# Early rows of x, late constant rows, and a new order in a planned attention layer

## The chip, the cores and the metric

The kernel runs on one core of a Trainium2 chip. The core has a matrix engine (TensorE, PE in the profile, with its weight loads shown apart as PEld), a vector engine (VectorE, DVE), a scalar engine (ScalarE, ACT), a general engine (GpSimd, POOL) and SyncE (SP), which issues the transfers between main memory and the core's own memory. The metric is device time in microseconds (us) from the first to the last instruction of one execution, with a little around it; lower is better.

## What is computed

The input x has 8 rows (batch) of 1024 tokens and 256 channels, all in float32. The layer is a chain of four blocks, each added to its input after a layer norm:

```python
x = x + retention(layernorm(x))     # 4 heads, dk 64, dv 128, gated, rotary, decay per head
x = x + ffn(layernorm(x))           # token shift, sigmoid(r) * (relu(k)^2 @ W_v)
x = x + attention(layernorm(x))     # 16 heads of 16, full softmax, bias by distance
x = x + ffn(layernorm(x))           # the same weights once more
```

The retention is a recurrent block. Per chunk of tokens, `attn = (q @ k.T) * Dmask` is applied to v, a state S of 64 x 128 per head carries what came before, the result is normed per head, gated with `g * sigmoid(g)` and multiplied by `Wo`. The feed-forward block mixes each token with the one before it, `xr = mu_r * x + (1 - mu_r) * x_prev` and the same for xk, and computes `sigmoid(xr @ W_r.T) * (relu(xk @ W_k.T)**2 @ W_v.T)`. The attention adds to each score a bias `rel_bias[bucket(distance)]`, which is the same for all keys far enough away, and takes a softmax over all 1024 keys.

## The kernel before

**Rows and chunks.** The eight rows go through the same functions, `retention(b)`, `ffn_front(b)`, `project_b(b)`, eight pairs of heads in `maxima(b, j)` and `shift(b, j)`, four groups of heads in `weigh(b, g)`, and `back(b)`. A row is cut into `NC = 4` chunks of `CT = 256` tokens; retention works on eight blocks of 128 tokens. `prepare(c)` loads a chunk of x and takes its moments; `turn_chunk(c)` norms it (tile z), turns it on PE and makes two float32r parts nT of it (line 912 writes the second, on DVE in the first row). A product that needs more than float32r's precision is three float32r matmuls of such parts (`mm3`, line 646); the projections qps, vps and gps of retention and qkp and bvp of attention are made so. The feed-forward and output products are plain float32.

**The attention** puts each head's queries and keys into stacks in main memory, `stk[0]` and `stk[1]`. Beside the 16 channels, a head's stack holds constant rows: for the queries, rows that say which key block a token may see as far (`c_stat`, copied from memory to memory by two transfers, lines 773 to 777), and for the keys, the same pattern times the head's far bias. The latter are worked out in the function `later()`: a tile `stat` is loaded, `d31` and `d0` hold two rows of the bias table, `fac` is made from them by a few small DVE instructions, and for each of the 16 heads DVE multiplies `stat` by a column of `fac` into a tile `kr` (line 798), which is stored into both parts of the key stack (line 800). The tiles stat and kr use the five buffers of the tag "k", the same as the key stacks loaded by `load_pair` later. `maxima` finds each query's greatest score, `weigh` computes the exponentials (tile e) and their products with the values (acc), and `back` divides by the sums, multiplies by the output weights (bop) and runs the second feed-forward block, `ffn_chunk(xt, b, c, "g", "")`.

**The feed-forward block** (`ffn_chunk`, line 1114) has one buffer each for zT, xk and xr per lane; the lane's name is the last argument. `ffn_front` uses the lane "f", `back` the lane "". In a chunk, the difference between a token and the one before is written into xk, then xr and xk are computed from it (lines 1130 to 1132), xk last and in place. kps is the keys' product, xk then takes its relu and its square, rps is the receptance product, whose tanh is written into xr, and yps the last product. xr then takes the product of both, and is added to x.

**The start.** SP's first transfers are a table of constants (cm), the norm's weights (ln), the four pieces of Wq and Wk (through the staging tiles xo, in `split`, which makes two float32r parts on ACT and DVE), and then the first chunk of x. `next_ones()` loads and splits Wv and Wg, loads Wo; `later()` loads all other weights and the constant rows.

**The order of the work** is not that of the text. Every operation is recorded (`Plan.record`) with an engine, an estimated cost and a target; `issue` then runs a clock of its own and lets each engine take, among the operations whose inputs are ready by that clock, the one with the lowest target (plus, for PE, penalties). What comes out is a fixed list for each engine, and the engines follow their lists in order. Targets run from -1 for the first row's retention up by one per row; `later()` is recorded at -0.9. Three things steer the order beside the targets: the estimate of a transfer,

```python
op.cost, op.tail = 0.4, 2.0 + size / 100000.0
```

the estimate of a matmul in `mm` (line 643), and the penalties. PE pays for a change in how its array is used ("rows" for the score products with 64 contracted rows, "cols", "acc", "all"). How much the choice counts such a change, and how much room for results it demands, is one of 16 `RULES`; the string `TURNS` names the rule, one hexadecimal digit for each 20 us of the planned clock.

```python
rule = RULES[int(TURNS[min(int(now / STRETCH), len(TURNS) - 1)], 16)]
change, least, pairs, later = rule[0], rule[1], rule[2], rule[3:]
```

Almost all instructions are emitted by `Plan.emit`, so the profile puts them at line 608; they are told apart by the names of their tiles. One plain float32 matmul appears as two instructions.

Of the kernel before, what the change touches and what calls it, by code (L numbers as in the profile page):

```python
# [76 lines left out]

STRETCH = 20
TURNS = (
    "00070270877472bf8931ef967bfe1d0522ff04383dfe37be3f1f7ef668e19e9c33271224f3e73df5"  # L80
    "5663e6176b19fd77763fbb3cafd79ff9fb9bf84111"
)
SWITCH = 0.1

# [227 lines left out]
class Plan:  # L312
# [66 lines left out]
    def record(self, eng, real, method, args, kw):  # L379
        cost = kw.pop("cost", None)  # L380
        views = [a for a in list(args) + list(kw.values()) if isinstance(a, View)]
        outs = [kw[k] for k in ("out", "accum_out") if isinstance(kw.get(k), View)]
        if "out" not in kw and isinstance(args[0], View):
            outs.append(args[0])
        if method in ("matmul", "transpose"):
            out, group = outs[0].t, kw.pop("group", None)
            op = self.last
            if op is None or op.group is not group or group is None and op.out[0] is not out:
                op = self.new(eng)
                op.out, op.cost, op.group = [], 0.0, group  # L390
                self.last = op
                k, m = args[1].shape[0], 1
                for n in args[1].shape[1:]:
                    m *= n
                op.mode = ("rows" if k == 64 and m == P else "cols") if k == 64 or m == 64 else "all"
                if out.tag == "acc":
                    op.mode = "acc"
                op.late = (0.055 if method == "transpose" else 0.1) if op.mode == "all" else 0.0
            if out not in op.out:
                op.out.append(out)  # L400
            op.cost += cost
        else:
            op = self.new(eng)
            n = 1
            for v in views:
                m = 1
                for d in v.shape[1:]:
                    m *= d
                n = max(n, m)
            if method == "dma_start":  # L410
                size = 4
                for d in (args[0] if isinstance(args[0], View) else views[0]).shape:
                    size *= d
                op.cost, op.tail = 0.4, 2.0 + size / 100000.0
            else:
                op.cost = self.estimate(eng, method, n, views, {
                    **kw, "op": args[3] if len(args) > 3 else None,
                    "scalar": len(args) > 2 and isinstance(args[2], View),
                })
                op.tail = AFTER[eng]  # L420
        op.calls.append((real, method, args, kw))
        for v in views:
            if v.t.space != "in":
                self.touch(op, v, any(v is o for o in outs))
        return op
# [186 lines left out]
def layer_kernel(ctx: ExitStack, tc: tile.TileContext, ap: dict, out: bass.AP):  # L612
# [26 lines left out]
    def mm(o, lhsT, rhs, start=True, stop=True, share=1.0, group=None):  # L639
        n = 1  # L640
        for d in rhs.shape[1:]:
            n *= d
        pe.matmul(o, lhsT, rhs, start=start, stop=stop, group=group,
                  cost=share * (0.004 + (4 if rhs.dtype == F32 else 1) * max(n, 64) / 2400.0))

    def mm3(o, lhsT, rhs, first, last):

# [24 lines left out]
    def split(w, names):  # L672
        for c in range(ND):
# [4 lines left out]
            act.copy(w[0][:, c], t)  # L678
            dve.tensor_tensor(w[1][:, c], t, w[0][:, c], ALU.subtract)

    split(wqk, ("a_Wq", "a_Wk"))
    wo_a = const([P, RH, D], "wo_a")
    gn = const([P, 1], "gn")
# [49 lines left out]
    def later():  # L733
        sp.dma_start(mu, ap["f_mu"])
        for k, t in wf.items():
            sp.dma_start(t, ap["f_" + k].rearrange("(c p) n -> p c n", p=P))

        dve.tensor_scalar(wf["W_v"], wf["W_v"], 0.5, None, ALU.mult)
        for k, w in wb.items():
            t = tile2k("xo0", 2).rearrange("p (c n) -> p c n", c=ND)  # L740
            sp.dma_start(t, ap["b_" + k].rearrange("(c p) n -> p c n", p=P))

            by = AHD**-0.5 if k == "wq" else 1.0
            act.activation(w[0], t, AF.Copy, scale=by)
            dve.scalar_tensor_tensor(w[1], t, by, w[0], ALU.mult, ALU.subtract)
        sp.dma_start(wo_b, ap["b_wo"].rearrange("(c p) n -> p c n", p=P))
        sp.dma_start(bqk, ap["b_bqk"])
        dve.tensor_scalar(bqk[:, 0, :], bqk[:, 0, :], AHD**-0.5, None, ALU.mult)

        rel = small([NBUCK, AH], "rel", 1)  # L750
        sp.dma_start(rel, ap["b_rel"])
        hot = tile2k("xo1", 2)
        sp.dma_start(hot[:NBUCK, :NU], ap["c_hot"])
        ups = misc("ups")
        mm(ups[:AH, :NU], rel, hot[:NBUCK, :NU])
        usb = tile2k("xo1", 2)
        dve.tensor_copy(usb[:AH, :NU], ups[:AH, :NU])
        sp.dma_start(ud, usb[:AH, :NU])


        bv, bo1 = small([P, ND], "bv", 1), tile2k("ob")[0:1, :D]
        sp.dma_start(bv, ap["b_bv"])
        sp.dma_start(bo1, ap["b_bo"])
        bps = misc("bps")
        for c in range(ND):
            mm(bps[0:1, :D], bv[:, c : c + 1], wo_b[:, c], c == 0, c == ND - 1)
        dve.tensor_tensor(bo1, bo1, bps[0:1, :D], ALU.add)
        sp.dma_start(bd, bo1)
        sp.dma_start(bo, bd.raw(0, [[0, P], [1, D]]))


        c_stat = ap["c_stat"]
        for i in range(2):
            sp.dma_start(
                stk[0][i, ROW_SHIFT // AHD],
                bass.AP(tensor=c_stat.tensor, offset=c_stat.offset, ap=[[0, AH], [T, AHD], [1, T]]),
            )
        stat = plan.tile([P, T], F32, "k", "stat", NJ)
        sp.dma_start(stat[:NSTAT], c_stat[1])
        far = small([NSTAT, NPART + 1], "far", 1)  # L780
        sp.dma_start(far, ap["c_far"])
        d31, d0 = small([NSTAT, AH], "d31", 1), small([NSTAT, AH], "d0", 1)
        sp.dma_start(d31, ap["b_rel"][NBUCK - 1].partition_broadcast(NSTAT))
        sp.dma_start(d0, ap["b_rel"][0].partition_broadcast(NSTAT))
        dve.tensor_tensor(d31, d31, d0, ALU.subtract)

        fac = small([NSTAT, AH], "fac", 1)
        dve.tensor_scalar(fac, d31, 0.0, far[:, NPART : NPART + 1], ALU.mult, ALU.add)
        for part in range(NPART):
            db = small([NSTAT, AH], f"db{part}", 1, F32R)  # L790
            dve.tensor_copy(db, d31)
            dve.tensor_tensor(d31, d31, db.bitcast(F32), ALU.subtract)
            dve.scalar_tensor_tensor(
                fac, db.bitcast(F32), far[:, part : part + 1], fac, ALU.mult, ALU.add
            )
        for h in range(AH):
            kr = plan.tile([P, T], F32, "k", "kr", NJ)[:NSTAT]
            dve.tensor_scalar(kr, stat[:NSTAT], fac[:, h : h + 1], None, ALU.mult)
            for i in range(2):
                sp.dma_start(stk[1][i, ROW_SHIFT // AHD, h], kr)  # L800

    def swift(alone):

# [70 lines left out]
    def retention(b):  # L874
        norms = {}

        def prepare(c):

            t = tile2k("xc", 4).rearrange("p (n d) -> p n d", n=2)
            sp.dma_start(t, rows_in(x[b], c))  # L880
            xc[b, c] = t
            mv = moments(t, "a")

# [230 lines left out]
    def ffn_chunk(xt, b, ch, name, own):  # L1114
# [11 lines left out]
        prev, cur = zT[:, :, 0:CT], zT[:, :, 1 : CT + 1]  # L1126
        xk = plan.tile([P, ND, CT], F32, "xk" + own, "xk", 1)
        xr = plan.tile([P, ND, CT], F32, "xr" + own, "xr", 1)
        eng.tensor_tensor(xk, cur, prev, ALU.subtract)
        for i, t in ((0, xr), (1, xk)):  # L1130
            for c in range(ND):
                dve.scalar_tensor_tensor(t[:, c], xk[:, c], mu[:, i, c : c + 1], prev[:, c], ALU.mult, ALU.add)
        lasts[name, b, ch] = small([P, ND, 1], name + "_last")
        pool.tensor_copy(lasts[name, b, ch], zT[:, :, CT : CT + 1])
        kps = misc("kps").rearrange("p (d t) -> p d t", d=ND)
# [34 lines left out]
    def project_b(b):  # L1170

        for ch in range(NC):
# [10 lines left out]
            for s, w in ((0, "wq"), (1, "wk")):  # L1183
# [15 lines left out]
                swift(b == 0).tensor_tensor(pt[1], res, pt[0], ALU.subtract)  # L1199
                t0 = (NC - 1 - ch if s == 0 else ch) * CT  # L1200
                for p, i in enumerate((Q_PARTS, K_PARTS)[s]):
                    sp.dma_start(rows_of(s, b, t0, p), pt[i].bitcast(F32))
            vps = misc("bvp")
            for i in range(2):
                for c in range(ND):
# [27 lines left out]
    def two(ps, q, k, qc, kc, queries):  # L1233

        group = object()
        for hh in range(2):
            r = slice(hh * HROWS, (hh + 1) * HROWS)
            a, m = (k[r, kc], q[r, qc]) if not queries else (q[r, qc], k[r, kc])
            mm(ps[hh] if isinstance(ps, list) else ps[:, hh, :], a, m, share=0.525, group=group)

    def near_bias(j, tag, bufs):

# [142 lines left out]
    def back(b):  # L1385

        for c in range(NC):
# [21 lines left out]
                       k == 0, k == ND - 1)  # L1409
            xf = xt.rearrange("p n d -> p (n d)")  # L1410
            dve.tensor_tensor(xf, xf, bps, ALU.add)
            ffn_chunk(xt, b, c, "g", "")
            sp.dma_start(rows_in(out[b], c), xt)


    for b in range(B):
# [3 lines left out]
            later()  # L1420
        ffn_front(b)
        project_b(b)
        for j in range(NPAIR):
            maxima(b, j)
            shift(b, j)
# [24 lines left out]
```

## Time and profile before

The median of the runs is 2560.08 us, the lowest 2556.73. The profiled execution took 2558.84 us, of which the span from the first to the last instruction is 2557.1.

| what | value |
|---|---|
| PE busy | 2474.7 us, 97% |
| DVE, ACT, POOL busy | 2108.6, 2071.8, 1592.5 us |
| mean granted clock of PE | 0.993 of full speed |
| DMA over the span | 251.17 MB, 98 GB/s |
| PE busy in 0 to 20, 20 to 40, 40 to 60 us | 2.91, 11.98, 14.82 us |
| PE busy in 2500 to 2520, 2520 to 2540, 2540 to the end | 15.69, 15.86, 8.27 us |
| first useful projection (qps) begins | 29.48 us |
| first query store (stk<-qk) is issued | 100.82 us |
| first loads of the stacks (q<-stk, k<-stk) are issued | 194.40 us |
| last value product (acc) ends | 2503.3 us |

A row of the timeline reads: start, duration (both in us), engine, line, operation, what it writes <- what it reads, shapes, and how many instructions are merged; in brackets, how long the engine was idle before and what ended the wait. A row of waits reads: who waited <- for whom: us in total, times, longest. A row of the chain reads: start, duration, what. Engines work beside each other, so that an engine's busy time is not the run's time; idle time counts where it is PE's.

### The profile page before, as it was taken

To read this page: it belongs to the slowest core of one execution; us is meant where nothing else is said; L and a number is where in the kernel's file an instruction comes from. 1 tells how busy PE (TensorE), PEld (TensorE's weight loads), DVE (VectorE), ACT (ScalarE), POOL (GpSimd) and SP (SyncE) were. 2 spreads that over 40 slices of the span, in tenths; PEclk is the share of its full clock that TensorE was granted. 3 is DMA by queue.
4 is the path that set the end of the run, shared out by engine and by line. 5 is a ranking of instruction groups with operands and counts; after the bars stand their busy time and mean duration, and the time that the engine had idled before them with its cause. 6 is when DMAs were issued, how large, how long until landed. Compare 5 with 4: busy or idle time off the path is not lost.

```text
span 2557.1 us, 51506 instructions
## 1 busy us (share of the span) xinstructions
PE 2474.7 (97%) x15814; PEld 1458.3 (57%) x15814; DVE 2108.6 (82%) x6230; ACT 2071.8 (81%) x5334; POOL 1592.5 (62%) x2675
## 2 busy tenths in 40 slices
PE   5999999999999999999999999999999999999997
PEld 3887755555555555555555555555555555554455
DVE  6767998888888888988888788888888888888855
ACT  3565598888989888988888889888898888787883
POOL 3467666666756666666657576666666566666642
PEclk9999999999999999999999999999999999999999
DMA  7136322444334333332324333324233344443322
GB/s 175 45 106 150 81 59 67 130 108 111 84 106 105 85 99 101 110 98 79 92 63 119 98 105 101 98 73 109 72 98 93 94 119 121 120 122 106 95 63 67
DMA packets 252225, 251.17 MB, mean 98 GB/s; under 512 B 89043, under 2 KB 226181, under 8 KB 251925
## 3 DMA queue, kind: packets, MB, share of 16 engines
q1 hardware_dynamic: 251956, 247.89, 36.6%
q8 instruction: 132, 2.16, 0.4%
q14 instruction: 137, 1.11, 0.2%
HBM read 151.32 MB, written 98.59 MB: 98 GB/s over the span
## 4 chain that ended last, share of the span: by engine, by line
PE 79%; DVE 9%; DMA 5%; ACT 4%; POOL 2%; issue 2%; SPq 1%; POOLq 0%; DVEq 0%; ACTq 0%
PE acc L608 16%; PE p L608 10%; PE s L608 10%; PE kps L608 4%; PE wps L608 4%; PE yps L608 4%; PE rps L608 4%; DVE pm L608 3%; PE qkp L608 3%; PE vps L608 3%; PE qps L608 3%; PE gps L608 3%; PE ops L608 3%; ACT e L608 2%; PE bop L608 2%
## 5 line engine op out<-in xcount | busy, mean ns | idle before, releaser
L608 DVE TENSOR_REDUCE pm<-p 128x1 f32<-128x512 f32 (+2 forms) x2048 | 1058.0, 558 | 84.9 <-PE p L608 83.1
L608 ACT ACTIVATE e<-s 128x512 f32<-128x512 f32 (+2 forms) x2048 | 1006.4, 526 | 54.9 <-PE s L608 51.8
L608 POOL TENSOR_TENSOR e<-e,hk 128x512 f32<-128x512 f32 (+1 forms) x558 | 615.0, 1109 | 344.9 <-ACT e L608 330.5
L608 PE MATMUL acc<-e,va 128*17 128x512 f32 x4096 | 529.0, 599 | 3.2 <-ACT e L608 2.9
L608 DVE CUSTOM_DVE_ANT_0 jmax<-p,hk 128x256 bf16<-128x256 f32 (+1 forms) x1152 | 428.1, 372 | 112.9 <-PE p L608 108.0
L608 PE MATMUL p<-k,q 64*128 64x512 f32 x2048 | 460.8, 439 | 5.4 <-DVE pm L608 3.1
L608 ACT COPY e<-s 128x256 f32<-128x256 f32 (+1 forms) x1116 | 398.9, 357 | 82.4 <-PE s L608 80.3
L608 PE MATMUL s<-q,k 64*128 64x512 f32 x2048 | 457.2, 438 | 5.4 <-DVE pm L608 3.3
L608 ACT ACTIVATE e<-e 128x512 f32<-128x512 f32 (+1 forms) x576 | 336.0, 586 | 56.4 <-POOL e L608 53.3
L608 PEld LDWEIGHTS p<-k,q 64*128 64x128 f32 x2048 | 207.9, 185 | 249.1 <-ACT e L608 95.2
L608 PEld LDWEIGHTS s<-q,k 64*128 64x128 f32 x2048 | 206.2, 185 | 204.4 <-issue 68.6
L608 PEld LDWEIGHTS acc<-e,va 128*17 128x17 f32 x4096 | 77.8, 95 | 189.0 <-issue 161.0
L608 PE MATMUL rps<-W_r,xr 128*128 128x256 f32 x512 | 127.7, 392 | 12.0 <-DVE xr L608 10.4
L608 PE MATMUL yps<-W_v,xk 128*128 128x256 f32 x512 | 126.9, 391 | 4.6 <-DVE xk L608 3.4
L608 PE MATMUL kps<-xk,W_k 128*128 128x256 f32 x512 | 128.1, 393 | 2.0 <-DVE xk L608 1.0
L608 PE MATMUL wps<-wo_a,gs 128*128 128x256 f32 x512 | 125.7, 388 | 0.6 <-ACT gs L608 0.5
L608 PEld LDWEIGHTS rps<-W_r,xr 128*128 128x128 f32 x512 | 93.3, 192 | 44.5 <-issue 12.4
L608 PE MATMUL qps<-wqk,nT 128*128 128x512 f32 x384 | 107.0, 414 | 6.0 <-DVE nT L608 5.5
L608 PEld LDWEIGHTS kps<-xk,W_k 128*128 128x128 f32 x512 | 94.3, 192 | 30.9 <-issue 10.7
L608 PEld LDWEIGHTS yps<-W_v,xk 128*128 128x128 f32 x512 | 93.1, 191 | 32.6 <-issue 12.1
L608 PEld LDWEIGHTS wps<-wo_a,gs 128*128 128x128 f32 x512 | 92.5, 190 | 26.5 <-issue 4.7
L608 POOL TENSOR_TENSOR ao_y<-ao_a,mhalf 128x4 f32<-128x4 f32 x64 | 65.7, 1027 | 66.6 <-DVE ao_a L608 65.9
(182 smaller groups left out, 4180.4 us busy)
## 6 DMA issues: line engine op xcount, KB each, us to landing
stk<-qk SPq DMA_DIRECT2D x192, 256.0 KB
hk<-ud SPq DMA_DIRECT2D x128, 256.0 KB
q<-stk SPq DMA_DIRECT2D x128, 256.0 KB
k<-stk SPq DMA_DIRECT2D x128, 256.0 KB
od<-o SPq DMA_DIRECT2D x64, 256.0 KB
vd<-vst SPq DMA_DIRECT2D x64, 136.0 KB
va<-vd SPq DMA_DIRECT2D x32, 272.0 KB
xc<-in_x SPq DMA_DIRECT2D x32, 256.0 KB
```

Of the source, the lines that this page charges most:

```text
L608: getattr(real, method)(*[be(a) for a in args], **{k: be(a) for k, a in kw.items()})
```

## The change

The first chunk of x is loaded by a transfer that is recorded ahead of the weights' (tile `first`). The constant rows of the stacks leave `later()` for a function `constant_rows()`, called after the first row's projections with the target -0.6, and all its transfers are planned behind the first query store (`stored[0]`). In the last row's `back`, odd chunks use the lane "f" and even ones the lane "", the difference is written into xr instead of xk, and xk is computed first. The plan's estimates change: transfers of operations with a target below -0.85 are taken to run at half the rate, float32r matmuls to cost n / 2270 us instead of n / 2400, and the pair of score products 0.5 of a matmul each instead of 0.525. The string of rules is another one. No other instruction is added or removed.

```diff
 TURNS = (
-    "00070270877472bf8931ef967bfe1d0522ff04383dfe37be3f1f7ef668e19e9c33271224f3e73df5"
-    "5663e6176b19fd77763fbb3cafd79ff9fb9bf84111"
+    "01721211a7731e138937018e991bcf6a3080107fffb91fb9013e97538778092d97bffb24e3e5d77e"
+    "efefa7f8fe786ec03266f72d4d1b1ff3f39caffb111"
 )
...
-                op.cost, op.tail = 0.4, 2.0 + size / 100000.0
+                op.cost, op.tail = 0.4, 2.0 + size / (50000.0 if self.target < -0.85 else 100000.0)
...
-                  cost=share * (0.004 + (4 if rhs.dtype == F32 else 1) * max(n, 64) / 2400.0))
+                  cost=share * (0.004 + (4 * max(n, 64) / 2400.0 if rhs.dtype == F32 else max(n, 64) / 2270.0)))
...
+    first = plan.tile([P, HALF], F32, "xc", "xc", 4)
+    sp.dma_start(
+        first.rearrange("p (n d) -> p n d", n=2), x[0][:CT, :].rearrange("(n p) d -> p n d", p=P)
+    )
     split(wqk, ("a_Wq", "a_Wk"))
...
+    stored = []
+
+    def constant_rows():
+
+        start = len(plan.ops)
+        plan.target = -0.6
         c_stat = ap["c_stat"]
...
+        for op in plan.ops[start:]:
+            if op.eng == "SP":
+                op.before.add(stored[0])
...
-            t = tile2k("xc", 4).rearrange("p (n d) -> p n d", n=2)
-            sp.dma_start(t, rows_in(x[b], c))
+            t = (first if b == c == 0 else tile2k("xc", 4)).rearrange("p (n d) -> p n d", n=2)
+            if b or c:
+                sp.dma_start(t, rows_in(x[b], c))
...
-        eng.tensor_tensor(xk, cur, prev, ALU.subtract)
-        for i, t in ((0, xr), (1, xk)):
+        diff = xr if name == "g" and b == B - 1 else xk
+        eng.tensor_tensor(diff, cur, prev, ALU.subtract)
+
+        for i, t in ((1, xk), (0, xr)) if diff is xr else ((0, xr), (1, xk)):
             for c in range(ND):
-                dve.scalar_tensor_tensor(t[:, c], xk[:, c], mu[:, i, c : c + 1], prev[:, c], ALU.mult, ALU.add)
+                dve.scalar_tensor_tensor(t[:, c], diff[:, c], mu[:, i, c : c + 1], prev[:, c], ALU.mult, ALU.add)
...
-                    sp.dma_start(rows_of(s, b, t0, p), pt[i].bitcast(F32))
+                    stored.append(sp.dma_start(rows_of(s, b, t0, p), pt[i].bitcast(F32)).n)
...
-            mm(ps[hh] if isinstance(ps, list) else ps[:, hh, :], a, m, share=0.525, group=group)
+            mm(ps[hh] if isinstance(ps, list) else ps[:, hh, :], a, m, share=0.5, group=group)
...
-            ffn_chunk(xt, b, c, "g", "")
+
+            ffn_chunk(xt, b, c, "g", "f" if b == B - 1 and odd else "")
...
         project_b(b)
+        if b == 0:
+            constant_rows()
```

## The prediction

> **What bounds the kernel now.** I read the page's engine rows first, then PE's own waits over the whole run, then the busy times by stage, and last the order of instructions at the two ends.
>
> ```profile
> span 2557.1 us, 51506 instructions
> PE 2474.7 (97%) x15814; PEld 1458.3 (57%) x15814; DVE 2108.6 (82%) x6230; ACT 2071.8 (81%) x5334; POOL 1592.5 (62%) x2675
> PE   5999999999999999999999999999999999999997
> ```
>
> PE is the bound: 97% busy, and in the slices only the first and the last are not full. All of PE's idle time is 2557.1 - 2474.7 = 82.4 us, which caps what a better order can bring, apart from changes of PE's own work. The waits say where the largest pieces lie (total, times, longest):
>
> ```profile
> PE bps L608 <- DMA bv<-in_b_bv: 17.0, 1, 17.0
> PE rps L608 <- DVE xr L608: 10.4, 6, 3.3
> PE qps L608 <- DVE nT L608: 5.5, 1, 5.5
> PE ops L608 <- ACT S L608: 5.2, 1, 5.2
> PE bop L608 <- POOL ob L608: 5.0, 1, 5.0
> ```
>
> Rows one, three and four are the head, row two is almost all the tail. By stage PE is busy 2.91 of the first 20 us, 11.98 of the second and 14.82 of the third: 30.3 us idle before 60 us. From 2500 to the end it is busy 15.69 + 15.86 + 8.27 = 39.8 of 57.1: 17.3 us idle. What is between, 60 to 2460 us, has 2365.45 of 2400 busy: 34.6 us idle in 2400.
>
> **The head: the first rows of x and the constant rows.** The order of the first useful matmul's inputs:
>
> ```profile
> 8.62 0.75 DVE L608 BATCH_NORM_STATS2 a_st<-xc 128x6 f32<-128x256 f32 x2
> ...
> 16.81 1.09 ACT L608 ACTIVATE z<-xc,a_nb,a_y 128x256 f32<-128x256 f32 x2
> ...
> 20.91 1.02 ACT L608 ACTIVATE z<-ntp,ln 128x256 f32<-128x256 f32 x2
> ...
> 25.66 0.16 DVE L608 TENSOR_TENSOR d<-d,d 16x16 f32<-16x16 f32 x1 [5.70 <-DMA d<-in_b_rel]
> ...
> 28.75 0.67 DVE L608 TENSOR_TENSOR nT<-z,nT 128x512 fp32r<-128x512 f32 x1
> ...
> 29.48 2.93 PE L608 MATMUL qps<-wqk,nT 128*128 128x512 f32 x6 [5.50 <-DVE nT L608]
> ```
>
> The second nT part needs z, ready at 21.93, but starts at 28.75: DVE stands for 5.70 us at the constant rows' first subtraction, whose two small loads were issued (17.94 to 18.96) behind two 1 MB copies of constant rows (14.31 and 16.28). That is 28.75 - 21.93 = 6.8 us, and these instructions leave the head. The step before it, z at 16.81, could have started when a_nb ended (13.89 + 0.20 = 14.09), but ACT stood at the second gate weight's load: 2.7 us. The doubled cost of early transfers makes the planner expect those weights later, so z should go first. The x load itself is SP's seventh issue (3.60) and becomes the third (1.70): 1.9 us earlier for x, and the four weight loads that it passes go 0.47 us later each. DVE read x at 8.62, directly behind the weight subtraction of 8.01 to 8.70; with x third it can read it at about 5.5 (the first pair of weight loads, issued at 2.18 to 2.61, was there at 5.59, about 3.0 us later). That is 3.1 us. Sum 6.8 + 2.7 + 3.1 = 12.6: the first projection at about 17 instead of 29.5.
>
> Less than that reaches the end. After 29.48 PE still idles 30.52 - 25.34 = 5.2 us up to 60, nearly all of it at ops, whose S copy stood on DVE behind constant rows; but with one row's retention alone its steps depend on each other, so I keep half of it and some 2 us of other waits (DVE still has weights to split, and stands 3.1 us at bqk). I take **-10 us**, with ends -2 (only x's earlier issue counts) and -15 (12.6 plus half of 5.2).
>
> PE's clock bears on this: from 50 to 60 us it is 0.75, behind the 5.2 us gap, and in the tail eight rps matmuls behind a 2.72 us gap take 3.38 us where those of the chunk before take 1.97. [...]
>
> **The same work, later.** Moved are 2 copies of 1 MB, 4 small loads, 32 stores of 64 KB (38 issues on SP), on DVE 16 kr at 0.734 = 11.7 us and eight small instructions, 1.5 us. They stand behind the first query store, issued at 100.82 before and some 10 us earlier now. Their deadline is far: the first q and k loads are at 194.4. In 95 to 145 us DVE is busy 35.3 of 50 and the DMA engines 0.40, so there is room; but PE has 48.75 of 50, and every DVE instruction there feeds it. The price is bounded below by 0 (all in DVE's 14.7 us of idle time). Above, take DVE standing 5.7 us at d once more, 0.8 at kr's buffers and half the 13.2 us of work in PE's way: 12. SP stood for kr 8.8 us in seven waits; the second chunk's stores and x loads (stk at 131, xc at 134) are queued behind, with some 30 us to spare. I take **+4**, nearer to the lower end because the rows on either side of the window show DVE at 70%.
>
> [...] POOL's 0.20 us steps take 0.63 at 2511.77, beside a DVE subtraction of two SBUF inputs. [...] No row shows a kr beside a busy POOL chain.
>
> **The tail: two lanes and keys first.** The chain that ended last:
>
> ```profile
> 2539.18 2.01 PE yps L608 x8
> ...
> 2542.54 0.69 DVE xk L608
> ...
> 2543.89 3.38 PE rps L608 x8
> 2547.27 1.74 PE kps L608 x8
> ...
> 2549.03 0.61 ACT xk L608
> ...
> 2549.66 0.70 DVE xk L608
> ...
> 2550.41 2.01 PE yps L608 x8
> ...
> 2553.17 0.69 DVE xo L608
> ```
>
> The last chunk's zT is ready at 2538.30 + 0.58 = 2538.88, but its xk waits until the third chunk is through yps, xr and xo: 2542.54. With its own buffers it starts 3.7 us earlier. Keys first put relu and square (0.61 + 0.70) beside rps: 1.3 us. Without the gap, rps is not at the slow clock: 1.4. Together 6.4. Further back, the third chunk's bop stood behind the first's yps (2521.22 against a product ready at 2519.94) and the last chunk's ftp behind kps (2537.60 against z at 2536.30): 1.3 each, of which I count half. Against it: the difference now lies in xr, which is free only after the final addition, not after yps; for the first chunk that is 2513.62 instead of 2511.66, but it is not on the path, since the third chunk waits for the sums' loads (2519.2). 6.4 + 1.3 = 7.7: **-8**, with ends -3 (the lane's 3.7 alone, less 0.7 should xr's wait reach the last chunk) and -9 (6.4 + 2.6).
>
> **The middle: new turns and rates.** The string picks one of 16 rules per 20 us of planned time; almost every instruction may stand elsewhere. Costs of two() hardly change: 0.525 x (0.004 + 512/2400) = 0.1141 becomes 0.5 x (0.004 + 512/2270) = 0.1148. Unshared float32r becomes 5% dearer in the plan, 0.2295 for 512 columns, and six of them measure 1.39 / 6 = 0.232. That is a truer plan, and no instruction is faster. What the rules steer is how often PE changes its array use: two s matmuls take 0.43, four 0.66, so a change costs 0.2. From PE's order I counted the changes per 20 us stretch from 360 to 2400 us: 15.5 to 18.0, by the old digit. The new digits with these means give 1694 changes against 1699: 1 us. So I take **0**. Bounds: the 34.6 us of idle time and some 14 us of slow clock (six 100 us stretches at 0.97 to 0.98) might shrink by 20, or grow by half, 25: they lie where a batch's transfers crowd (DMA share 0.82 at 2190 to 2200, bop idle 5.0, clock 0.76) and where the new order meets them is open.
>
> **Sum.** -10 + 4 - 8 + 0 = -14. The profiled execution took 2558.84 us (span 2557.1 and 1.7 around it), so 2544.8; the median of the runs is 1.2 us above it, which is less than I can claim. Forecast **2545**.
>
> **Rivals.** (1) *The middle gains too*, as the truer plan keeps PE fed: the same ends and -20 in the middle, 2525. For it: 48 us are lost there; against: the count of changes stands still. (2) *Slower than before*: PE, which takes its instructions in order, meets transfers that land later than planned, at the joints of the batches. Price by the place at 2190 to 2202: 5.0 us idle, then bop 3.80 instead of 1.92, and the clock still 0.90 in the next 10 us: 8 us each. Six such dips of the clock exist now (at 1220, 1430, 1530, 2070, 2190 and 2340); two more eat the 14 us, four more give 2545 + 32 = 2577, and it decides from the second on. (3) *The x load doesn't do what it says*: z stays behind weights on ACT and nT behind other waits on DVE, as it stood behind bqk and ups; the head gives -2, the moved rows cost 4, the tail 8: 2553.
>
> Chances: forecast 0.55 (2530 to 2556 with its own bounds), (1) 0.18, (2) 0.17, (3) 0.10. The range takes in (1), (3) and the nearer half of (2): 2520 to 2570. A difference under 2%, 51 us, can hardly be told from none in measurements of this kernel: faster than that 0.04, within 0.92, slower 0.04.
>
> **What would show it.** In the profile after, the first qps near 17 us and the first 60 us with some 20 us idle; no d or kr on DVE before 80 us, and PE no worse than 97% busy from 90 to 140; kps ahead of rps in the last chunks, and the last xo ending some 43 us behind the last acc, where it is 2553.9 - 2503.3 = 50.6 now. I am wrong if PE stands near 100 us for DVE, or if idle time between 60 and 2460 us moves by over 20 us.

## The result and the profile after

The change made the kernel a little slower: 2569.54 us median of five runs (2564.97 to 2579.0) against 2557.68 before, a ratio of 1.0053 with a 95% interval of 1.0034 to 1.0071; the ratio leaves out one of the five runs of before, 2720.51 us, which was in a slower state. That is 9 to 18 us more, where 14 fewer were forecast. The profiled execution took 2564.97 us, of which the span is 2563.3.

The page of the kernel after, its span, the engines' busy times and PE's slices:

```profile
span 2563.3 us, 51511 instructions
PE 2481.1 (97%) x15814; PEld 1463.0 (57%) x15814; DVE 2108.7 (82%) x6230; ACT 2069.4 (81%) x5334; POOL 1590.5 (62%) x2675
PE   6899999999999999999999999999999999999997
```

PE's idle time is 82.2 us, as before (82.4), and PE is busy 6.4 us longer for the same 15814 matmuls. So idle time changed its place. The mean granted clock is 0.993 in both, so the page alone doesn't say which matmuls took longer; from 100 to 150 us the clock is 0.90, where it was 1.00. The first slice is fuller (6 where it was 5). PE's waits in the kernel after (total, times, longest):

```profile
PE bps L608 <- DMA bv<-in_b_bv: 15.3, 1, 15.3
...
PE wps L608 <- DVE xr L608: 5.5, 1, 5.5
PE qps L608 <- DVE nT L608: 5.0, 2, 3.3
PE kps L608 <- DVE xk L608: 4.8, 5, 2.1
PE bop L608 <- DVE ob L608: 3.2, 1, 3.2
```

The wait of ops for S (5.2) and the large ones of rps for xr are gone; wps for xr and bop's wait for DVE's ob are new. To see where the time went I cut each trace at four marks, which lie at the same work in every kernel: the first query store, the first load of a stack, the end of the last acc, the end of the span.

| us | before | after | difference | forecast |
|---|---|---|---|---|
| start to first query store | 100.82 | 92.89 | -7.9 | -10 (head) |
| to the first load of a stack | 93.6 | 109.6 | +16.0 | +4 (moved rows) |
| to the end of the last acc | 2308.9 | 2302.4 | -6.5 | 0 (middle) |
| to the end | 53.8 | 58.4 | +4.6 | -8 (tail) |

One profile is not exact by this table. Kernels that share the lists of all engines up to the last row differ in the middle by 5 us (2303.4 in e1 below, 2308.9 before). Over all profiles of this study but two, e4 and e11, the middle is 2302 to 2313 us; the nine in the new order have a mean of 2307.0, the four in the old one 2306.0. So I count the middle as 1, and the first, second and last row carry the result: -7.9 + 16.0 + 1 + 4.6 = 13.7. The two profiles as they stand differ by 6.2, as the profiled run of after is the fastest of its five; the timed difference of 9 to 18 takes in the first of these sums and not the second.

**The head.** The timeline after, rows that answer those shown of before:

```profile
8.75 0.74 DVE L608 BATCH_NORM_STATS2 a_st<-xc 128x6 f32<-128x256 f32 x2
...
13.35 1.09 ACT L608 ACTIVATE z<-xc,a_nb,a_y 128x256 f32<-128x256 f32 x2 [3.47 <-POOL a_nb L608]
...
19.15 1.02 ACT L608 ACTIVATE z<-ntp,ln 128x256 f32<-128x256 f32 x2
...
20.72 0.68 DVE L608 TENSOR_TENSOR nT<-z,nT 128x512 fp32r<-128x512 f32 x1
...
21.46 2.93 PE L608 MATMUL qps<-wqk,nT 128*128 128x512 f32 x6 [3.26 <-DVE nT L608]
```

The stand at d is gone (nT starts 0.55 after z ends, where it was 6.8), z went ahead of the weights (13.35 for 16.81), but x is read no earlier (8.75 for 8.62). The first store and the first qps both come 8 us sooner.

**The stretch behind the first query store.** First the chain, its longest pieces; then the timeline (SPq are SP's issues):

```profile
102.18 8.26 DMA d<-in_b_rel
...
111.84 2.73 DVE kr L608 x4
...
136.60 6.47 DMA xc<-in_x
...
145.74 3.46 PE rps L608 x8
```

```profile
98.76 1.26 SPq L608 DMA_DIRECT2D stk<-in_c_stat  x2
...
101.16 1.34 SPq L608 DMA_DIRECT2D d<-in_b_rel  x2
...
110.54 0.17 DVE L608 TENSOR_TENSOR d<-d,d 16x16 f32<-16x16 f32 x1 [6.90 <-DMA d<-in_b_rel]
...
112.61 14.24 SPq L608 DMA_DIRECT2D stk<-kr  x24
...
115.31 3.69 PE L608 MATMUL wps<-wo_a,gs 128*128 128x256 f32 x8 [5.51 <-DVE xr L608]
...
118.89 0.19 POOL L608 TENSOR_SCALAR b_mv<-b_mv 128x2 f32<-128x2 f32 x1 [12.75 <-DVE b_mv L608]
...
128.06 4.49 SPq L608 DMA_DIRECT2D stk<-kr  x8
...
136.60 1.31 SPq L608 DMA_DIRECT2D xc<-in_x  x1
```

The stand at d moved with the constant rows and grew: the small loads were again issued behind the two 1 MB copies. DVE stood 6.90 us, with four kr and xr behind d in its list; PE stood 5.51 for xr, and its next eight matmuls took 3.69 at a granted clock of 0.53 (from 2529.2 to 2538, at 1.00, eight take 1.89). POOL stood 12.75. The 32 stores held SP, and the next chunk of x was issued at 136.60, 43.7 us behind the first query store, where before it was issued at 133.97, 33.2 behind it. DVE then waited 3.09 us for it.

**The tail.** The chain that ended last, and the timeline behind the last acc (it ends at 2504.91):

```profile
2550.33 3.75 PE kps L608 x8
2554.09 2.70 PE rps L608 x8
2556.78 1.74 PE yps L608 x8
...
2559.35 0.69 DVE xo L608
```

```profile
2504.84 1.99 PE L608 MATMUL bop<-wo_b,ob 128*128 128x256 f32 x8
...
2511.72 3.56 PE L608 MATMUL bop<-wo_b,ob 128*128 128x256 f32 x8 [3.15 <-DVE ob L608]
...
2531.83 0.69 DVE L608 TENSOR_TENSOR ob<-ob,os 128x512 f32<-128x512 f32 x1
...
2538.27 1.89 PE L608 MATMUL bop<-wo_b,ob 128*128 128x256 f32 x8
```

The lanes and keys first are there, but the first chunk's bop stands behind the last acc (before: ahead of it, 2499.43 against 2503.27), and the last chunk's bop starts 33.4 us behind the last acc, 24.4 before, though its input was ready at 2532.52. The last kps and rps take 3.75 and 2.70, at granted clocks of 0.50 and 0.64.

### The profile page after: what moved, and what is told of

The parts are those of the page before. It is cut to its first block, busy times and chain, and to the rows that moved or that the text cites. A ratio compares the mean times of both kernels' runs of the same rounds, so it can differ in the third digit from the quotient of the medians.

```text
span 2563.3 us, 51511 instructions
## 1 busy us (share of the span) xinstructions
PE 2481.1 (97%) x15814; PEld 1463.0 (57%) x15814; DVE 2108.7 (82%) x6230; ACT 2069.4 (81%) x5334; POOL 1590.5 (62%) x2675
## 4 chain that ended last, share of the span: by engine, by line
PE 78%; DVE 10%; DMA 5%; ACT 3%; POOL 2%; issue 1%; SPq 1%; DVEq 0%; POOLq 0%; ACTq 0%
PE acc L608 16%; PE p L608 10%; PE s L608 10%; PE kps L608 4%; PE yps L608 4%; PE wps L608 4%; DVE pm L608 4%; PE rps L608 4%; PE qps L608 3%; PE gps L608 3%; PE vps L608 3%; PE ops L608 3%; PE qkp L608 3%; ACT e L608 2%; PE bop L608 2%; DVE xr L608 1%
## 5 line engine op out<-in xcount | busy, mean ns | idle before, releaser
L608 ACT ACTIVATE e<-s 128x512 f32<-128x512 f32 (+2 forms) x2048 | 1010.0, 531 | 54.5 <-PE s L608 52.7
L608 PEld LDWEIGHTS wps<-wo_a,gs 128*128 128x128 f32 x512 | 93.6, 192 | 29.1 <-issue 8.5
L608 PE MATMUL vps<-wv_a,nT 128*128 128x512 f32 x384 | 106.3, 413 | 0.2 <-DVE pm L608 0.2
```

What stands on the lines that cost most here:

```text
L608: getattr(real, method)(*[be(a) for a in args], **{k: be(a) for k, a in kw.items()})
```

## The experiments

All ratios are against the kernel before. Where it says that an order is kept, the planner's order stands, and only the named operations are emitted elsewhere.

### Parts of the change alone

**e1**: the kernel before with `diff` and the lane "f" of the change in the last row, nothing else.

> The kernel before with the two lanes and the keys first in the last row alone; the planned order of all that comes earlier is that of before. Theory A (the lanes help, and the tail of the changed kernel was lost to the new string and rates): the last chunk's chain shortens by the 5 to 8 us of the prediction, ratio to before 0.997 to 0.998, span from the end of the last acc to the end 46 to 49 us instead of 53.8. Theory B (the lanes themselves cost, because with two chunks open PE and DVE take the output product of the last chunk after both): no gain or a loss of up to 5 us, ratio 1.000 to 1.002, last acc to end 54 to 59 us, and the last bop starts at least 5 us later behind the last acc than the 24.3 us of before.

Measured 0.9988 (0.9977 to 0.9998), 3.1 us by the ratio; from the last acc to the end 53.0 for 53.8 (51.3 and 51.1 in e9 and e15 below, which have the same lists there). The lanes help in the old order, by less than half of what I took.

**e4** has the new string and the new estimates, **e11** the new estimates with the old string.

```diff
# e4: the string TURNS of after, and as in e11:
-                op.cost, op.tail = 0.4, 2.0 + size / 100000.0
+                op.cost, op.tail = 0.4, 2.0 + size / (50000.0 if self.target < -0.85 else 100000.0)
-    ... share * (0.004 + (4 if rhs.dtype == F32 else 1) * max(n, 64) / 2400.0))
+    ... share * (0.004 + (4 * max(n, 64) / 2400.0 if rhs.dtype == F32 else max(n, 64) / 2270.0)))
-            ... share=0.525
+            ... share=0.5
```

> The kernel before with the new string of turns and the new rates alone (x, constant rows and last row as before). Theory A (the moved rows cause the loss from 90 to 160 us): PE is idle there no more than 3 us, the head loses only what the doubled cost of early transfers gives or takes (first qps 26 to 30 us), the middle gains the 6 us that lie between the first stack loads and the last acc, and the time is 0 to 8 us under before, ratio 0.997 to 1.000. Theory B (the new order itself brings the loss): over 6 us of PE's idle time between 90 and 160 us without any moved row, ratio 1.003 to 1.006.

> The kernel before with the new estimates (early transfers, float32r, the pair of score products) and its old string of turns. Theory A (a string fits only the list of operations and costs for which it was chosen, so that any new plan with an unfitted string is some per cent worse): 50 to 130 us slower than before, ratio 1.02 to 1.05, as with the new string on the old operations (1.049). Theory B (the new string is bad for the old operations, and the estimates are harmless): within 15 us of before, ratio 0.995 to 1.006.

Measured: e4 1.0486 (1.0469 to 1.0503), e11 1.0401 (1.0382 to 1.042). The page of e11:

```profile
span 2654.1 us, 51461 instructions
PE 2529.6 (95%) x15814; PEld 1470.3 (55%) x15814; DVE 2109.5 (79%) x6230; ACT 2070.3 (78%) x5334; POOL 1595.4 (60%) x2675
```

PE has 54.9 us more of busy time and 42 more of idle time for the same matmuls, over the whole middle. The new estimates cost 4% by themselves, though float32r's is nearer to the measured duration (for 512 columns 0.2295 us, before 0.217; measured 0.232). The old string beside the new estimates and the new string beside the old operations both do badly; the new string with the old estimates was not run. In the changed kernel, string, estimates and list together bring the middle back to where it was. My middle of 0 was right, but by the whole set.

**e10**: the kernel after with the first x load emitted seventh on SP, as before.

```diff
     sp.dma_start(first...)          # recorded first
+    plan.late.add(len(plan.ops) - 1)
+    # emitted when the loads of split(wqk, ...) are out
```

> The changed kernel with the first chunk of x issued behind the four pieces of Wq and Wk again, all else as planned. Theory A (the early load gives nothing, as DVE reads x behind the weight subtractions either way: 8.75 us in the changed kernel, 8.62 before): first qps within 0.5 us of 21.5, the same time as the changed kernel, ratio 1.004 to 1.007. Theory B (it gives the 1 to 3 us that were predicted): first qps at 22.5 to 24.5, ratio 1.005 to 1.008.

Measured 1.0038 (1.0024 to 1.0053); first qps at 21.40 (after: 21.46). The early x load brings nothing that can be seen. With it the weights come later, and DVE reads x at 8.75 behind their subtractions; without it the subtractions are done at 7.43, and DVE waits 0.51 for x and reads it at 7.94.

**e7**: the kernel after with the last row in one lane and keys last.

> The changed kernel with the last row in one lane and keys last, as before; all earlier is as in the changed kernel. Theory A (lanes help, the new string hurts): undoing the lanes costs another 5 to 8 us, ratio to before 1.007 to 1.009, last acc to end 63 to 66 us. Theory B (two lanes hurt): it gains 2 to 6 us, ratio 1.002 to 1.004, last acc to end 52 to 56 us.

Measured 1.0078 (1.0063 to 1.0093), 6.4 us above after; from the last acc to the end 68.9 for 58.4. In the profiles it is 10.5, more than the 0.8 to 2.7 of the old order. Without the lanes the new order's tail is 15 us longer than that of before (53.8).

### The moved rows

**e6**: the kernel after with the two copies emitted behind the four small loads. **e8**: besides, one constant row per four DVE instructions instead of several at once. **e12**: e6 without most kr.

```diff
         for op in plan.ops[start:]:
             if op.eng == "SP":
                 op.before.add(stored[0])
+        moved = [op.n for op in plan.ops[start:] if op.eng == "SP"]
+        plan.late.update(moved[:2])       # the copies: held until
+        plan.loads.update(moved[2:6])     # these are out
+        plan.rows.update(...)             # e8 alone: the rest, three at a time
+        plan.same.update(...)             # e12 alone: 12 kr not emitted
```

> The changed kernel with one thing altered in SP's list: the two 1 MB copies of constant rows stand behind the four small loads instead of ahead of them; all other lists are as planned. Theory A (DVE's stand of 6.9 us at d, behind the copies, is the larger part of the loss between 90 and 160 us): DVE's wait at d falls below 2 us, PE's idle time from 100 to 150 us falls from 11.7 to about 6, with the slow clock of that stretch gone too, and the time falls by 6 to 9 us, to a ratio of 0.998 to 1.001 to before. Theory B (the kr instructions, SP's 32 stores and the transfers behind them are what costs): DVE's wait is gone but PE stands elsewhere, less than 3 us gained, ratio 1.003 to 1.005.

> The changed kernel with its planned order kept, the two copies behind the four small loads, and in addition the constant rows' DVE instructions and stores put in one at a time, about one kr behind every four to five other DVE instructions, instead of four at a stretch. Theory A (what the loads left of the loss is kr standing in bunches on DVE ahead of work that PE waits for): PE idle from 100 to 150 us falls from the 6.3 us with the loads first to about 3, first stack loads at 188 to 191 us, 4 to 7 us under the run with the loads first, ratio to before 1.000 to 1.002. Theory B (the transfers of the rows beside the others are what costs): first stack loads stay near 195 us, ratio 1.003 to 1.004.

> The changed kernel with the copies behind the small loads, as in the run with the loads first, and 12 of the 16 kr multiplications left out (the constant key rows of heads 4 to 15 are then those of heads 0 to 3, so the far bias of these heads is another head's); all 32 stores stay. It asks what of the remaining loss is DVE's time at kr. Theory A (DVE's work): 8.8 us of it go, the stretch from the first query store to the first stack loads falls from 101.7 us to 94 to 96, and the time by 5 to 8 us, ratio to before 0.998 to 1.001. Theory B (stores, copies and SP's list): the stretch stays at 99 us or more, ratio 1.002 to 1.004.

Measured: e6 1.0037 (1.0022 to 1.0051), e8 1.0015 (1.0004 to 1.0026), e12 1.0027 (1.0017 to 1.0037); first query store to first stack load 101.7, 101.0 and 103.9. DVE's waits of e6 from 85 to 165 us:

```profile
DVE d L621 <- DMA d<-in_b_rel: 0.9, 1, 0.9
```

The same loads, ahead of the copies on the same queue, cost 0.9 instead of 6.9. The stretch is 7.9 us shorter than in after, and 5.9 shorter than the mean of four profiles with after's lists up to there (107.6). The timed ratios give 4, but their intervals overlap. Leaving out 12 of 16 kr, 9 us of DVE, made the stretch no shorter and the ratio only 0.001 lower, which the intervals don't tell apart; PE's waits of e12 from 95 to 190 us say why:

```profile
PE sps L627 <- DVE a_mv L627: 6.6, 1, 6.6
```

a_mv needs the next chunk of x, whose load SP issued at 132.64, behind the 32 stores that were still there: 38.5 us behind the first query store, as in e6 (38.3). PE came there sooner and waited. So the rows cost by SP's queue as well as by DVE's list.

What stayed open here was whether the rest of e8's stretch, 101.0 against 93.6, is still the rows or the new order. Two runs with the rows in the other place, in each order, decide. **e14**: the kernel after, its order kept, with the rows taken out of the stretch and emitted early and spread. **e15**: e1, its order kept, with the rows emitted behind the first query store, as far behind it as in after.

```diff
# e14, in the order of after
+                take = 6 if seen == 18 else 3 if seen >= 38 and seen % 4 == 2 else 0
# e15, in the order of before: other DVE instructions behind the first query store
+    at = [9, 9, 11, 12, 14, 14] + [19] * 8
+    for n in (19, 19, 19, 19, 23, 23, 24, 26, 30, 30, 30, 31, 34, 34, 34, 34): at += [n] * 3
```

> The kernel after with its order kept on every engine, but the constant rows taken out of the stretch behind the first query store: their four loads, the two copies, and then one row per four DVE instructions stand early, from the 18th DVE instruction on. Theory A (the lump of rows costs about 8.6 us of the stretch's 16, and the new order itself the other 7.4): first qps about 22.5, first query store to first stack load about 101, as with the rows spread; ratio 1.0015. Theory B (every microsecond of the 16 is the moved rows, spread or not): the stretch is back at 93.6, ratio 0.999.

> The kernel before with the last row in two lanes, its order kept on every engine, but the constant rows emitted behind the first query store as in the kernel after: the two copies 9 other DVE instructions behind it, the four loads 11 to 14, the small instructions 19, and the sixteen rows from 19 to 34. Theory A (lump 8.6, order 7.4): first qps about 22, first query store to first stack load about 102 (93.2 and 8.6), ratio 0.999. Theory B (the rows cost 16 in any order): the stretch is about 109, ratio 1.002.

Measured: e14 1.0013 (1.0001 to 1.0024), stretch 93.6; e15 1.0011 (1.0002 to 1.002), stretch 112.6. My theory A falls: the new order costs nothing there. (e14's ratio is the one that theory A gave, but for another reason: the rows cost some 4 us at their early place, and the tail's loss stays.) The busy times of both from 100 to 150 us, first e14, then e15 (us, PE with its count, PEld, DVE, ACT, POOL, PE's clock, DMA share, GB/s; before, PE had 48.75):

```profile
100.00:150.00 50.00, 49.22 (x306) 41.04 (x305) 35.71 (x86) 26.80 (x59) 29.07 (x72) 1.00 0.36 84
```

```profile
100.00:150.00 50.00, 32.63 (x196) 27.15 (x195) 33.36 (x74) 18.22 (x40) 21.80 (x45) 0.83 0.72 134
```

And PE's waits of e15, where DVE's stand of 8.5 at d and nine kr lie ahead of the xk that PE needs:

```profile
PE yps L628 <- DVE xk L628: 15.2, 1, 15.2
```

With these, each place of the rows has its price in us, against the same order with no rows in that part. It is worked out from one to seven profiles each, and profiles of equal lists differ by up to 3.5 us, so that entries as near as 7.9 and 7.2 aren't told apart:

| rows | old order | new order |
|---|---|---|
| early, at once | 11.2: first store at 101.2 (before, e1) against 89.94 (e15) | not run |
| early, spread | 4.9: 94.85 (e9) against 89.94 | 4.4: 97.3 (e14, e16) against 92.9 (the seven with late rows) |
| late, behind the copies | 19.2: 112.6 (e15) against 93.4 (before, e1, e9) | 13.8: 107.6 (after, e7, e10, e13) against 93.8 (e14, e16) |
| late, loads first | not run | 7.9: 101.7 (e6) |
| late, spread | not run | 7.2: 101.0 (e8) |

**e9**: the kernel before, its order kept, with the copies behind the loads, the rows spread from the twelfth DVE instruction behind them on, and the lanes of e1.

> The kernel before with its planned order, the constant rows early as there, but the copies behind the small loads and the rows' DVE instructions and stores put in one at a time from the twelfth DVE instruction on, and the last row in two lanes. Theory A: nT no longer stands behind d, first qps at 23 to 25 us instead of 29.5, the stall at ops near 50 us goes, no loss later, and the lanes give their 3 us: 8 to 12 us under before, ratio 0.995 to 0.997. Theory B (the head is bound by other waits, and a kr costs the same wherever it stands): first qps at 27 us or later, ratio 0.998 to 0.999, the lanes' share alone.

Measured 0.9955 (0.9941 to 0.9969), 2546.82 us: this version beats both kernels. Its page and its first projection, which waits 1.36 where it waited 5.50:

```profile
span 2546.6 us, 51509 instructions
```

```profile
22.68 2.93 PE L638 MATMUL qps<-wqk,nT 128*128 128x512 f32 x6 [1.36 <-DVE nT L638]
```

The first query store is at 94.85, the stretch is 93.3, and the tail 51.3. The timed ratios fit this table in sign and rough size: e14 gains 10 us on the kernel after (9.4 by the table), e8 10 (6.6), e6 4 (5.9); e9 gains 8 on e1 (6.3), and e15 loses 6 (8.0). Most of the change's gain in the head, 6.0 of 7.9 us at the first store, is to be had without moving the rows out of it.

### The tail's order

**e13**: the kernel after with a lower target for the last row's output products; on PE this moves one thing, the last bop. **e16**: e13 and e14 together.

```diff
+            plan.target -= 1.0 * (b == B - 1)
             swift(b == B - 1).tensor_tensor(oT, oT, sm, ALU.mult)
...
             dve.tensor_tensor(xf, xf, bps, ALU.add)
+            plan.target += 1.0 * (b == B - 1)
```

> The kernel after, with one thing moved: the last chunk's output product (bop) stands in PE's list ahead of yps, rps, yps and ftp of the two chunks before it, not behind them; all other lists of PE are the same. In the profile of after its input is there at 2532.52 and it starts at 2538.27. Theory A (the tail lost to the new order on PE): it starts about 2532.7, 5.6 us earlier, and of that some 4 us reach the end, because the third chunk's products come 1.7 later: last acc to end about 54 instead of 58.4, ratio to before 1.0037. Theory B (the tail is held by the long steps on DVE, POOL and ACT of the shared lane): the last chunk waits for its buffers anyway, tail 58, ratio 1.0053.

> Both edits together in the kernel after: the constant rows early and spread, the last output product ahead. By the theories A the ratio is 1.0015 - 0.0016 = 1.000; if the rows are the whole price of the stretch and the tail is as it is, 0.999; if both parts are back, 0.9975.

Measured: e13 1.0046 (1.0029 to 1.0063), e16 1.0012 (1.0 to 1.0025); from the last acc to the end 55.9 in both, 2.5 and 2.7 us less than in after and e14. PE's timeline of e13:

```profile
2534.01 1.89 PE L608 MATMUL bop<-wo_b,ob 128*128 128x256 f32 x8
...
2547.43 1.89 PE L608 MATMUL yps<-W_v,xk 128*128 128x256 f32 x8
2549.16 0.60 PE L608 MATMUL ftp<-cm,z 128*128 128x128 f32 x4
2552.11 1.97 PE L608 MATMUL kps<-xk,W_k 128*128 128x256 f32 x8 [2.36 <-DVE xk L608]
2553.92 1.89 PE L608 MATMUL rps<-W_r,xr 128*128 128x256 f32 x8
```

bop starts 5.8 us sooner behind the last acc (27.6 for 33.4), but the last ftp then stands behind the third chunk's yps in the list, and the last kps starts 45.7 us behind the last acc, where it was 45.4 in after. So the place of bop doesn't hold the tail. The 2.5 us are the last kps and rps, which take 1.97 and 1.89, where in after, at granted clocks of 0.50 and 0.64, they took 3.75 and 2.70. The timed ratios show no sure gain either: each interval holds both its expectation and no gain at all.

Such longer products hide the order in the other tails too. In before and after they stand at granted clocks of 0.50 to 0.64; at 1.00 products of eight matmuls take 1.97 to 1.99 us behind a gap there and 1.89 without one. As an estimate, I put the whole excess in every tail down to the clock and take from each what its products of eight took beyond 1.97 behind a gap, or 1.89 without one. The durations are those of PE's timeline of each run. This leaves:

| from the last acc to the end, us | as measured | without the low clock |
|---|---|---|
| old order, one lane (before) | 53.8 | 52.4 |
| old order, two lanes (e1, e9, e15) | 53.0, 51.3, 51.1 | 47.8, 47.9, 47.6 |
| new order, one lane (e7) | 68.9 | 62.0 |
| new order, two lanes (after, e6, e8, e10, e12, e14) | 57.1 to 58.6 | 53.9 to 54.0 |
| the same, bop ahead (e13, e16) | 55.9 | 54.5 |

By this the lanes are worth 4.6 us in the old order and 8.0 in the new one, and the new order costs 6 to 10. What in it makes the tail longer I have only read in the trace: the first bop behind the last acc, and with it the load of the single ob buffer (issued at 2506.87, before at 2501.46), at which PE stands 3.15 us and then needs 3.56, at a granted clock of 0.55, for a product of 1.89. That wasn't tried and stays open.

## Why the prediction was wrong

The time lies just inside the upper end of the range, 2570, but the sign of the change was wrong. Two steps failed, by some 10 to 13 us each: the price of the moved rows and the tail. Step by step:

- **What bounds the kernel** held: PE is 97% busy before and after, and every loss found is a wait of PE or its clock behind one.
- **The head, -10**, measured -7.9. The 6.8 us of DVE's stand at d and the z behind the weights went as described (first 60 us with 20.7 us idle; some 20 were forecast). The 3.1 for the earlier x load failed: the load is issued third, but DVE still reads x at 8.75 behind the weight subtractions, and e10 shows no loss without it. So the first qps is at 21.46 and not near 17. The end of -2, at which only x's earlier issue counts, was the wrong way about: that piece gave nothing, and the others came.
- **The moved rows, +4, is the first step that failed.** They cost 16.0 in this profile and 13.8 in the mean of the profiles with these lists (e15: 19.2 in the old order). I had the pieces: the stand at d once more, 5.7, and "half the 13.2 us of work in PE's way". I set them as an upper bound of 12, which even the mean exceeds, and took a value near the lower end, where all of the work lies in DVE's 14.7 us of idle time. That idle time is no cover. Before, the order had PE at 48.75 of 50 in this stage, so DVE's gaps were waits for PE and ACT (5.9 us for qk, 3.7 for gs), not room; when d waited for its loads in the middle of DVE's list, all behind it waited too, 6.90 us in after and 8.54 in e15, and PE stood 5.51 and 15.18. I also wrote that the small loads stood behind two 1 MB copies, and moved both together, but the +4 doesn't let the stand move with them. And "some 30 us to spare" on SP was wrong: in after DVE waits 3.09 us for the x load behind the stores, and in e12 PE waits 6.6.
- **The tail, -8, is the second step that failed**: measured +4.6. The lanes were right in kind: -3.1 us in the old order (e1), -6.4 in the new one (e7), by the timed ratios. In the old order they were over-sized. The 1.4 us of clock that I counted as gained went the other way: the tails of e1, e9 and e15 lose 3.4 to 5.2 us to the low clock, by the estimate above, where before lost 1.4. The larger part is what I left out, that the new string and estimates reorder the tail as well as the middle: e7 has 68.9 where before has 53.8. I gave the middle bounds of -20 and +25 for the new order, and the tail none. What in the new order makes the tail longer stays open.
- **The middle, 0**, held: 2307.0 against 2306.0 in the means. That it could have been +100 (e4, e11) none of my bounds said.
- **The rivals.** (2), slower, comes near the mechanism, PE standing at transfers that come late for a list, but at another place and by way of DVE's list: not at the joints of the batches, but where the rows were put. (3), the x load doing nothing, was right about x and wrong about the rest of the head.
- **POOL beside DVE** doesn't explain the price of the moved rows. POOL stood 12.75 us idle for DVE's b_mv in that stretch; of the eight small steps that begin there, two took 0.63 and 0.67 instead of 0.20 and one 0.87 instead of 0.70, about 1 us together. On DVE, of the sixteen kr two took 1.21 and 1.77 us instead of 0.74, beside POOL's addition to xc and its nT. No run shows what makes them longer.

What would have shown it, in numbers: PE from 100 to 150 us has 38.32 of 50, the sign that I had named for being wrong ("PE stands near 100 us for DVE"); the last xo ends 55.1 us behind the last acc, not 43.

## What to carry to other kernels

Work that is moved takes its waits along. Before counting idle time of an engine as room, ask what the moved instruction waits for at its new place, and what stands behind it on that engine and on the queue that feeds it: here putting four small loads first took 5.9 of 13.8 us off the price in the profiles, while leaving out 9 of the 11.7 us of arithmetic took nothing off, since the stores still held the queue. Often the cure is in place: order the small loads ahead of the large copies and spread the work between other instructions (e9, 0.9955), instead of moving it.

A rule string like TURNS may fit only one list of operations with one set of estimates. The old string with new estimates cost 4.0% here, and the new string and estimates with the old operations 4.9%. And a new order is new everywhere, at the ends too, so each end needs its own bounds.

## What the runs showed of the hardware

- Two loads of a row of 16 values each, issued behind two 1 MB copies on the same queue, took 8.3 us to land in after's chain (issued 101.16 to 102.50, used at 110.54); ahead of the copies they took 4.2 in e12's, and in e6 they were issued 100.56 to 101.49 and used at 105.26.
- Whether a gap of PE cost clock didn't go by its length alone. In before, eight matmuls took 1.97 us behind gaps of 3.34 and 2.14, at a granted clock of 1.00, and 3.38 behind 2.72, at 0.55; behind 2.38 and 2.36 they took 1.97 (e13). Behind 2.14 us at the end of after, eight kps matmuls took 3.75 and the next eight 2.70, at 0.50 and 0.64; this gap cost in all six profiles with that end (3.35 to 3.75), and there another gap of 1.05 and only four short products lie just ahead of it. No run shows what decides it.
- Without a change of the program's lists up to there, the stretch of some 100 us behind the first query store differed by up to 3.5 us between profiles (106.1 to 109.6 in e13, e7 and after), and the middle of 2300 us by up to 5.5. A cut of one profile is no better than that; only the timed rounds tell a difference of 0.2%.
